# A list planner that counts column loads of W longer and joins the two halves of some DMA transposes

## The chip, the cores and the metric

The kernel runs on one core of a Trainium2 chip, in one launch. Its time is in device microseconds; lower is better. Five instruction queues of the core matter here: TensorE (PE) for matmuls, VectorE (DVE), ScalarE (ACT), GpSimd (POOL), and SyncE (SP), which does no arithmetic and issues every DMA of the kernel.

## What is computed

For each of two batches, `x` is 1024 x 2048 and `ctx` is 2048 x 2048, both float32:

```python
x = x + _L0_xattn_ref(_layernorm(x, axis=-1), ctx_4096, L0_xattn_x1_scale, ...)
x = x + _L0_ffn_ref(_layernorm(x, axis=-1), L0_ffn_W_base, L0_ffn_b_base, ...)
```

The first step quantizes both operands to 8 bits with a scale and a zero point, brings them back, and multiplies them (1024 x 2048 by 2048 x 2048). The second is a linear layer with W (2048 x 2048) and a bias, plus a mixture of 8 experts of rank 16: a router takes the softmax of 8 logits for each token, keeps the best two, and the weighted low-rank products are added.

## The kernel before: tiles, stages and its planner

**The work.** 128 tokens make a tile, so a batch has 8 tiles, worked on in 4 pairs p. Batch 0's first matmul (line 755, into banks `g`) is plain; batch 1's (line 875, `gX` and `gY`) and the FFN matmul of both batches (line 1320, `X` and `Y`) use Strassen's scheme with 7 products of half matrices in place of 8. The FFN operands are each split into two float16 parts, high and low, and three products of parts are summed, so line 1320 issues three matmuls of 128 x 512 a step. The FFN is walked in blocks: for the column half cp of W (f = 0, 1), for the group grp (0 to 3) of Strassen products, for the row block k (0 to 7) of W, for the pair p.

**y.** After the first matmul, `ln2` and `y_prep` (lines 888 to 977) make the seven half sums of normalized x (`yt_...`), split each into a high part by a cast (line 939) and a low part by a subtraction (line 942) in `nat_...` (shape 128 x 2 x 1024), and turn each part by a DMA transpose on SP (`transpose`, line 385) into `y_...`. In the profile the seven appear as `nat_a`/`y_a` and `nat_s`/`y_s`. The low part is made from the high part, so its transpose can be issued one subtraction later at the earliest. Both readers of y, `g2` (line 1311) and `hmm` (line 979, banks `ph`), need both parts. Two other places transpose in two halves: `ln1` for tiles 4 to 7 of batch 0 (`at<-qn`), and `router` (`hT<-hh`). Batch 1's `q<-q` is one transpose for a tile already.

**W.** `w_step` (line 1108) loads what a block needs of W, forms the Strassen combination on VectorE, casts it on ScalarE or VectorE (`affine`, line 396) with the scale gW, and makes the low part on VectorE (line 1130). Row loads, `load_wrow` (`wt`, `wb`), take 128 rows of 1024 consecutive values. Column loads, `load_wcol` (line 570), take the same 512 KB as two pieces of 512 values from two row blocks: `wc` for groups 0 and 2 of f = 0, and all 16 `wn` loads of each `w_norm` (line 579). `w_norm(cp)` squares and sums a column half of W on ScalarE or VectorE (lines 591 and 593), adds the partitions by a matmul (`wsum`, line 604), and computes gW and the factors that undo it (lines 610 to 617, on VectorE); no cast of that half of W can start before.

**The planner.** The program doesn't issue in source order. Each call of `plan.add` makes a Task with its engine (or a choice of ScalarE and VectorE), a modelled duration, what it reads and writes, and for matmuls a due time. `rank` (line 158) passes due times back to predecessors, taking off the duration and a slack (3.0 for a DMA); the modelled DMA time isn't in it. `order` (line 171) then simulates the queues with these numbers, picks for each free engine the ready task with the earliest due time whose buffers fit, and finally sorts all tasks by modelled start. Each engine then runs its part of the list strictly in that order, and semaphores make it wait where the chip differs from the model.

A DMA of n bytes a partition is modelled as `n * 128 / RATE` on one shared channel (`dma_free`), with 0.42 us on SP, landing 2.1 us (`LAND`) after its channel time. SP issues a DMA only while the channel is booked at most `DEPTH` = 2.5 us ahead and fewer than 8 transfers are in flight (`lanes`). A transpose of a half is 1.5 us on SP and 1.0 on the channel; transfers in flight take places of a ring of 5, a half takes 2, and SP is held until there is room:

```python
if t.turn:
    room = RING - TURN_RING
    for at, n in sorted(lanes, reverse=True):
        room -= n
        if room < 0:
            end = max(end, at)
            break
```

Of the kernel before, what the change touches and what calls it, by code (L numbers as in the profile page):

```python
# [22 lines left out]
P = 128  # L23
# [10 lines left out]
C = 512  # L34
NC = O // C
HD = D // 2
# [45 lines left out]
HOP = 0.7  # L82
DMA_SLACK = 3.0
RATE = 374e3
LAND = 2.1
STORE_LAND = 1.15
TURN_LAND = 0.65
TURN_COST = 1.0
TURN_ISSUE = 1.5
RING = 5  # L90
TURN_RING = 2
NEXT = {"DVE": 0.08, "ACT": 0.1}

# [14 lines left out]
class Task:  # L108
    __slots__ = ("eng", "dur", "durs", "fn", "preds", "succs", "prio", "cap", "bufs", "left",
                 "ready", "start", "done", "dma", "seq", "pe", "far", "need", "turn",  # L110
                 "store")


class Plan:
# [4 lines left out]
    def add(self, eng, dur, fn, r=(), w=(), prio=None, cap=None, dma=None, far=None, turn=False,  # L119
            store=False):  # L120
        t = Task()
        t.durs = eng if isinstance(eng, dict) else {eng: dur}
        t.eng, t.dur = None, min(t.durs.values())
        t.fn, t.prio, t.cap, t.dma = fn, prio, cap, dma
        t.preds, t.succs, t.bufs = set(), [], []
        t.seq, t.ready, t.start, t.done = len(self.tasks), 0.0, None, None
        if self.lead is not None:
            t.cap = self.lead
        t.pe = prio if eng == "PE" else None
        t.far, t.turn, t.store = far, turn, store  # L130

        def spans(accs):
            for a in accs:
                buf, parts = a if isinstance(a, tuple) else (a, None)
                if buf not in t.bufs:
                    t.bufs.append(buf)
                    buf.users += 1
                for i in range(buf.parts) if parts is None else parts:
                    yield buf, i

        for buf, i in spans(r):
            last, readers = buf.state[i]
            if last is not None:
                t.preds.add(last)
            readers.append(t)
        for buf, i in spans(w):
            last, readers = buf.state[i]
            if last is not None:
                t.preds.add(last)
            t.preds.update(readers)  # L150
            buf.state[i] = (t, [])
        t.preds.discard(t)
        for p in t.preds:
            p.succs.append(t)
        self.tasks.append(t)
        return t
# [14 lines left out]
    def order(self):  # L171
        self.rank()
        free = dict(SLOTS)
        busy = dict.fromkeys(("SP", "ACT", "DVE", "POOL", "PE"), 0.9)
        ready = {e: [] for e in busy}
        events = [0.0, 0.9]
        lanes = []
# [45 lines left out]
        while todo:  # L223
            if not events:
                raise RuntimeError("no progress")
            nxt = heapq.heappop(events)
            if nxt <= now:
                continue
            now = nxt
            while releases and releases[0][0] <= now:  # L230
                free[heapq.heappop(releases)[-1].tag] += 1
            for eng in busy:
                while busy[eng] <= now:
                    pick = None
                    q = ready[eng]
                    for n, item in enumerate(q):
                        t = item[2]
                        if t.ready > now:
                            continue
                        h = t.far if t.far is not None else HORIZON  # L240
                        if t.prio + lag > now + h:
                            wake(t.prio + lag - h)
                            if t.prio + lag > now + HORIZON:
                                break
                            continue
                        if t.dma is not None:
                            if dma_free > now + DEPTH:
                                wake(dma_free - DEPTH)
                                break
                            if len([x for x in lanes if x[0] > now]) >= LANES:  # L250
                                break
                        if (eng == "DVE" and len(t.durs) > 1 and busy["ACT"] <= now
                                and t.prio > -100):
                            continue
                        if not fits(t):
                            continue
                        pick = t
                        break
                    if pick is None:
                        break  # L260
                    t = pick
                    t.eng, t.dur = eng, t.durs[eng]
                    for e in t.durs:
                        ready[e].remove((t.prio, t.seq, t))
                    for tag, n in t.need.items():
                        free[tag] -= n
                        queue[tag].remove(t)
                    held.update(t.bufs)
                    t.start = now
                    end = now + t.dur  # L270
                    if t.dma is not None:
                        if t.turn:
                            room = RING - TURN_RING
                            for at, n in sorted(lanes, reverse=True):
                                room -= n
                                if room < 0:
                                    end = max(end, at)
                                    break
                        dma_free = max(end + 0.2, dma_free) + t.dma
                        t.done = dma_free + (  # L280
                            TURN_LAND if t.turn else STORE_LAND if t.store else LAND
                        )
                        lanes = [x for x in lanes if x[0] > now]
                        lanes.append((t.done, TURN_RING if t.turn else 1))
                    else:
                        t.done = end + 0.1
                        end -= NEXT.get(eng, 0.0)
                    busy[eng] = end
                    wake(end)
                    wake(t.done)  # L290
                    if t.pe is not None:
                        lag = now - t.pe
                    for b in t.bufs:
                        b.users -= 1
                        if b.tag in free:
                            b.last = max(getattr(b, "last", 0.0), t.done)
                            if not b.users:
                                heapq.heappush(releases, (b.last, next(count), b))
                                wake(b.last)
                    for s in t.succs:  # L300
                        s.left -= 1
                        s.ready = max(s.ready, t.done)
                        if not s.left:
                            for e in s.durs:
                                bisect.insort(ready[e], (s.prio, s.seq, s))
                            wake(s.ready)
                    todo -= 1
        return sorted(self.tasks, key=lambda t: (t.start, t.seq))


@with_exitstack
def xattn_ffn_kernel(ctx, tc, x, cx, scal, wT, bias, arT, bT, out):
# [65 lines left out]
    bmax_b = fixed(None)  # L378
    scale_b = fixed(None, 2)

    def load(dst, dst_ap, src, nbytes, w, r=(), **kw):
        add("SP", 0.42, lambda: nc.sync.dma_start(dst_ap(), src() if callable(src) else src),
            r=r, w=w, dma=nbytes * P / RATE, **kw)

    def transpose(dst, src, r, w, cols, **kw):
        add("SP", TURN_ISSUE, lambda: nc.sync.dma_start_transpose(dst(), src()),
# [183 lines left out]
    def load_wcol(k, cp, c, n, **kw):  # L570
        s = buf("u", [P, HD], F32, n)
        o = cp * HD + c * C
        load(s, lambda: s.ap().rearrange("p (h c) -> p h c", h=2),
             wT.rearrange("(h k p) n -> k p h n", h=2, p=P)[k][:, :, o : o + C], HD * 4, [s], **kw)
        return s

    kept = {}
# [61 lines left out]
    def ln1(S, b, i):  # L639
# [46 lines left out]
        else:  # L686
# [10 lines left out]
            if not pe_turn:  # L697
                for h in range(2):
                    transpose(
                        lambda h=h: aT.ap()[:, h * HK : (h + 1) * HK, :],  # L700
                        lambda h=h: qn.ap()[:, h * HD : (h + 1) * HD], [(qn, [h])], [(aT, [h])],
                        HD)
        S["at", i] = aT
        if first:
            warm = bank("warm")
# [26 lines left out]
    def load_b(S, b, c):  # L732
        for j in range(4):
            bp = buf("u", [P, 4, C], F16, f"b_{b}_{c}_{j}", 2)
            S["b", c, j] = bp
            for h in range(2):
# [2 lines left out]
                s = buf("u", [P, 2, C], F32, f"bs_{b}_{c}_{j}_{h}")  # L739
                load(s, s.ap,  # L740
                     cx[b, k0 * P : (k0 + 2) * P, c * C : (c + 1) * C].rearrange(
                         "(p k) n -> p k n" if b else "(k p) n -> p k n", p=P), HD * 4, [s])
                u = buf("u8", [P, 2, C], U8, f"u_{b}_{c}_{j}_{h}")
                affine(u.ap, s.ap, HD, [s], [u], scale=r2, bias=z2)
                affine(lambda bp=bp, h=h: bp.ap()[:, h * 2 : h * 2 + 2, :], u.ap, HD, [u],
# [174 lines left out]
    def y_prep(S, b, p):  # L920
# [10 lines left out]
        def emit(o, t):  # L931
# [4 lines left out]
            def turn_half(a):  # L936
# [6 lines left out]
                    n.ap()[:, 1], t.ap(), n.ap()[:, 0], ALU.subtract),  # L943
                r=[t, (n, [0])], w=[(n, [1])])
            turn_half(1)

        def comb(dst, a, c, op):
            add("DVE", 1.22, lambda: nc.vector.tensor_tensor(dst.ap(), a.ap(), c.ap(), op),  # L948
# [63 lines left out]
    def router(S, b):  # L1012
# [71 lines left out]
        for q in range(2):  # L1084
# [2 lines left out]
                lambda ts=ts: hT.ap()[:, ts].rearrange("p t h c -> p (t h) c"),  # L1087
                lambda ts=ts: hh.ap()[:, ts].rearrange("p t h c -> p (t h c)"),
                [hh], [(hT, [q])], HD)

    made = {}
    STORED = {
# [413 lines left out]
```

## Time and profile before

| What | us |
|---|---|
| median of 3 runs | 927.42 |
| lowest and highest run | 926.86, 928.04 |
| profiled execution | 927.01 |
| its span, first to last instruction | 925.2 |
| busy in the span: TensorE, VectorE, ScalarE, GpSimd | 901.1, 708.7, 404.3, 66.1 |
| mean granted TensorE clock | 0.991 |

The profile shows one execution. Busy time is what an engine spent on its instructions, without waits. Names in it are the program's tiles without their numbers; `X L1320` is an instruction of line 1320 that writes tile X. "A <- B: t, n, m" in a view of waits says that A waited t us for B in n places, at most m at once. A row of the timeline is: start, length, engine, line, operation, tiles, count of instructions in a row, and the idle time before. `SPq` is SP's queue: the length of a DMA there is the time that SP was held by issuing it, not the transfer's.

The DMA queue's issues, with the median time from issue to landing in us (the first lines and the transposes):

| Transfer | Count | KB | Issue to landing |
|---|---|---|---|
| bs<-in_cx_dram | 64 | 512 | 10.0 |
| wt<-in_wT_dram | 64 | 512 | 7.3 |
| wn<-in_wT_dram | 32 | 512 | 8.8 |
| wc<-in_wT_dram | 16 | 512 | 6.9 |
| y_s<-nat_s (transpose) | 64 | | 3.5 |
| y_a<-nat_a (transpose) | 48 | | 3.6 |
| at<-qn, q<-q, hT<-hh (transposes) | 8, 8, 4 | | 4.5, 6.3, 3.7 |

### The profile page before, as it was taken

The page shows a single profiled execution, that of the slowest core. Times are in us where ns is not written, and L with a number is a line of the kernel's source. Part 1 is how long each engine was busy: PE and PEld are TensorE (multiplying, and loading weights), DVE is VectorE, ACT ScalarE, POOL GpSimd, SP SyncE. Part 2 cuts the span into 40 slices and gives each one's busy share as a digit, 9 for nine tenths or more (in the row PEclk, how much of TensorE's full clock was granted, in tenths as well). Part 3 has the DMA queues.
Part 4 walks back from the last instruction along what each step waited for, and adds up shares of the span by engine and source line. Part 5 has one row for each costly group of instructions (what it writes and reads, how often), then busy time and mean ns, then how long its engine had stood idle before and what let it go on. Part 6 is the DMA issues. An engine that isn't in the chain of part 4 may idle for free.

```text
span 925.2 us, 12515 instructions
## 1 busy us (share of the span) xinstructions
PE 901.1 (97%) x4514; PEld 432.4 (47%) x4514; DVE 708.7 (77%) x1264; ACT 404.3 (44%) x461; POOL 66.1 (7%) x256
## 2 busy tenths in 40 slices
PE   7999998999999899999999999899999999999998
PEld 5444444474444344444444444546544444444443
DVE  7998899989497874989898997799745354799131
ACT  5999677415064331313597575852300011234000
POOL 0023120000000000001552002000000000000000
PEclk8999998999999999999999999999999999999999
DMA  9999999997999999999999656999997159793021
GB/s 322 386 385 295 314 295 253 172 237 228 224 329 322 341 357 405 336 400 353 323 351 314 201 202 171 242 190 187 298 216 255 57 179 385 267 352 126 12 87 49
DMA packets 224526, 241.03 MB, mean 261 GB/s; under 512 B 146640, under 2 KB 158928, under 8 KB 224464
## 3 DMA queue, kind: packets, MB, share of 16 engines
q1 hardware_dynamic: 224464, 240.24, 85.6%
q8 instruction: 35, 0.57, 0.2%
q14 instruction: 27, 0.22, 0.1%
HBM read 163.65 MB, written 41.94 MB: 222 GB/s over the span
## 4 chain that ended last, share of the span: by engine, by line
PE 71%; DVE 11%; DMA 10%; ACT 4%; issue 2%; POOL 1%; SPq 1%; DVEq 0%; ACTq 0%
PE X L1320 30%; PE Y L1320 24%; PE g L755 6%; DMA wn<-in_wT_dram 4%; PE ph L989 2%; PE gX L875 2%; DMA q<-q 2%; PE gY L875 2%; DVE x L784 2%; PE X L1336 1%; PE ph L993 1%; PE Y L1336 1%; DMA lbs<-in_bT_dram 1%; ACT at L396 1%; DMA wb<-in_wT_dram 1%
## 5 line engine op out<-in xcount | busy, mean ns | idle before, releaser
L1320 PEld LDWEIGHTS <-y_s 128*128 128x128 f16 x1536 | 150.2, 98 | 181.8 <-issue 1.3
L1320 PE MATMUL X<-w,y_s 128*128 128x512 f16 x768 | 206.8, 379 | 0.8 <-DVE w L1130 0.8
L1320 PE MATMUL Y<-w,y_s 128*128 128x512 f16 x768 | 206.8, 379 | 0.0
L1320 PE MATMUL X<-w,y_a 128*128 128x512 f16 x768 | 191.8, 382 | 6.5 <-DVE w L1130 2.6
L1320 PEld LDWEIGHTS <-y_a 128*128 128x128 f16 x1152 | 113.0, 99 | 142.0 <-issue 12.1
L755 PE MATMUL g<-b,at 128*128 128x512 f16 x512 | 113.6, 381 | 4.4 <-ACT at L396 2.3
L1320 PE MATMUL Y<-w,y_a 128*128 128x512 f16 x384 | 104.5, 383 | 0.0
L396 ACT ACTIVATE w<-wb,gW 128x1024 f16<-128x1024 f32 (+1 forms) x47 | 50.3, 1073 | 120.3 <-DVE wb L1191 46.2
L1348 DVE SCALAR_TENSOR_TENSOR xr<-X,uW,xr 128x512 f32<-128x512 f32 x64 | 46.7, 746 | 44.0 <-PE X L1336 24.0
L755 PEld LDWEIGHTS <-at 128*128 128x128 f16 x512 | 49.8, 98 | 64.0 <-issue 3.4
L1130 DVE SCALAR_TENSOR_TENSOR w<-wb,gW,w 128x1024 f16<-128x1024 f32 (+1 forms) x48 | 57.1, 1193 | 8.9 <-ACT w L396 8.8
L1348 DVE SCALAR_TENSOR_TENSOR xr<-Y,uW,xr 128x512 f32<-128x512 f32 x42 | 31.1, 744 | 34.8 <-PE Y L1336 34.6
L396 ACT ACTIVATE b<-u,nz 128x1024 f16<-128x1024 uint8 x40 | 44.7, 1138 | 14.5 <-DVE bt L846 13.8
L446 POOL TENSOR_TENSOR sm<-sm 128x1 f32<-128x1 f32 (+1 forms) x48 | 12.2, 253 | 490.0 <-DVE sm L432 484.0
L396 ACT ACTIVATE w<-wt,gW 128x1024 f16<-128x1024 f32 x16 | 18.0, 1145 | 64.5 <-DVE wt L1177 40.0
L419 DVE BATCH_NORM_STATS2 sm<-x 128x6 f32<-128x512 f32 x64 | 40.9, 682 | 3.1 <-DMA x<-in_x_dram 3.0
L396 ACT ACTIVATE q<-x,sm 128x1024 uint8<-128x1024 f32 x30 | 35.9, 1228 | 12.1 <-POOL sm L655 6.5
L396 ACT ACTIVATE nat_s<-yt_a 128x1024 f16<-128x1024 f32 x28 | 28.8, 1051 | 27.9 <-DVE yt_a L948 23.9
L803 ACT ACTIVATE sq<-x,sm 128x1024 uint8<-128x1024 f32 x32 | 36.4, 1137 | 10.4 <-DVE x L784 10.3
L396 ACT ACTIVATE yt_a<-x,sm 128x1024 f32<-128x1024 f32 x26 | 31.1, 1232 | 20.4 <-POOL sm L916 12.1
L396 ACT ACTIVATE u<-bs,sc,rec 128x1024 uint8<-128x1024 f32 x31 | 38.0, 1232 | 4.3 <-DMA bs<-in_cx_dram 3.6
L875 PEld LDWEIGHTS <-at 128*128 128x128 f16 x256 | 24.9, 98 | 30.9 <-issue 1.4
(189 smaller groups left out, 1177.9 us busy)
## 6 DMA issues: line engine op xcount, KB each, us to landing
bs<-in_cx_dram SPq DMA_DIRECT2D x64, 512.0 KB, 10.0
wt<-in_wT_dram SPq DMA_DIRECT2D x64, 512.0 KB, 7.3
wn<-in_wT_dram SPq DMA_DIRECT2D x32, 512.0 KB, 8.8
x<-in_x_dram SPq DMA_DIRECT2D x30, 512.0 KB, 8.5
spill<-x SPq DMA_DIRECT2D x28, 512.0 KB, 3.6
xr<-spill SPq DMA_DIRECT2D x28, 512.0 KB, 8.3
wb<-in_wT_dram SPq DMA_DIRECT2D x24, 512.0 KB, 8.0
out_dram<-xr SPq DMA_DIRECT2D x24, 512.0 KB, 5.8
```

The source lines that it names most:

```text
L396: nc.scalar.activation(o, i, AF.Copy if c is None else AF.Identity, scale=1.0 if a is None else a, bias=0.0 if c is None else c,)
L419: nc.vector.bn_stats(st[:, 2 * h + c], b.ap()[:, c * C : (c + 1) * C])
L446: e.tensor_tensor(t, r, r, ALU.mult)
L755: nc.tensor.matmul(ps.ap(), aT.ap()[:, k, :], S["b", c, k // 4].ap()[:, k % 4, :], start=k == 0, stop=k == KT - 1,)
L784: nc.vector.scalar_tensor_tensor(xs, ps.ap(), s12, xs, ALU.mult, ALU.add, **kw)
L803: nc.scalar.activation(sq.ap(), xb.ap(), AF.Square, bias=a[:, 22 + j : 23 + j], accum_out=a[:, 24 + 2 * j + h : 25 + 2 * j + h],)
L875: nc.tensor.matmul(ps.ap(), a()[:, 4 * h + k, :], w.ap()[:, k, :], start=fresh and h + k == 0, stop=h == 1 and k == 3, skip_group_check=True,)
L989: nc.tensor.matmul(ph.ap()[:, : 2 * AR], y[half].ap()[:, 0, k, :], ar[:, kr, :], start=kk == 0, stop=False,)
L1130: lambda: nc.vector.scalar_tensor_tensor(w.ap()[:, 1, lo:up], src(), g, w.ap()[:, 0, lo:up], ALU.mult, ALU.subtract),
L1320: nc.tensor.matmul(ps.ap(), y.ap()[:, a, k, :], w.ap()[:, q, j * C : (j + 1) * C], start=k == 0 and fresh and i == 0, stop=k == HK - 1 and ...
L1336: nc.tensor.matmul(ps.ap(), hT.ap()[:, 2 * p + tt, a], lb.ap()[:, q], start=fresh and i == 0, stop=i == 2, skip_group_check=True,)
L1348: nc.vector.scalar_tensor_tensor(xs, ps.ap(), uW[:, cp : cp + 1], xs, ALU.mult, ALU.add)
```

## The change

It has two parts, both in the planner and in what it is told.

1. `load` gets a factor `slow` on the modelled channel time of a DMA: 1.18 for column loads of W (`load_wcol`), 1.03 for loads of cx in `load_b`.
2. The last two transposes added before a call of `pair_up` become mates, with a function that issues one DMA transpose for both halves. When one of them is picked, its mate is ready too, the mate's buffers are held (or are the same), and every transfer in flight lands within `MERGE` = 2.5 us by the model, the two are issued as one: 1.8 us on SP (and SP held until the last transfer in flight has landed), twice the channel time, 4 places of the ring. `pair_up` is called in `ln1`, `y_prep` and `router`.

The core of the diff:

```diff
+SLOW_W = 1.18
+SLOW_C = 1.03
+MERGE = 2.5
+WHOLE_ISSUE = 1.8
...
+                    group = [t]
+                    m = t.mate
+                    if m is not None and m.start is None and not m.left and m.ready <= now:
+                        ok = all(b in held or b in t.bufs or b.tag not in free for b in m.bufs)
+                        if ok and max([x[0] for x in lanes] or [0.0]) < now + MERGE:
+                            group.append(m)
+                            t.dur = WHOLE_ISSUE
+                            t.fn, m.skip = t.whole, True
                     end = now + t.dur
                     if t.dma is not None:
                         if t.turn:
-                            room = RING - TURN_RING
+                            room = RING - TURN_RING * len(group)
                             for at, n in sorted(lanes, reverse=True):
                                 room -= n
-                                if room < 0:
+                                if room < 0 or len(group) > 1:
                                     end = max(end, at)
                                     break
-                        dma_free = max(end + 0.2, dma_free) + t.dma
+                        dma_free = max(end + 0.2, dma_free) + t.dma * len(group)
...
-    def load(dst, dst_ap, src, nbytes, w, r=(), **kw):
+    def load(dst, dst_ap, src, nbytes, w, r=(), slow=1.0, **kw):
         add("SP", 0.42, lambda: nc.sync.dma_start(dst_ap(), src() if callable(src) else src),
-            r=r, w=w, dma=nbytes * P / RATE, **kw)
+            r=r, w=w, dma=nbytes * P / RATE * slow, **kw)
+
+    def pair_up(whole):
+        a, c = [t for t in plan.tasks[-3:] if t.turn][-2:]
+        a.mate, c.mate = c, a
+        a.whole = c.whole = whole
...
+            pair_up(lambda: nc.sync.dma_start_transpose(
+                y.ap().rearrange("p h k t -> p (h k) t"), n.ap().rearrange("p h c -> p (h c)")))
```

The rest of the diff books the group's two tasks together (start, end, buffers, successors) and leaves the skipped one out of the final list.

More of the change, by code (lines that the diff above doesn't have):

```diff
@@ L110 @@
                  "ready", "start", "done", "dma", "seq", "pe", "far", "need", "turn",
-                 "store")
+                 "store", "whole", "mate", "skip")
 class Plan:
@@ L130, in add @@
         t.far, t.turn, t.store = far, turn, store
+        t.whole = t.mate = None
+        t.skip = False
         def spans(accs):
@@ L262, in order @@
                     t.eng, t.dur = eng, t.durs[eng]
[L263 to L269, printed above, removed]
+                    group = [t]
[6 more added lines that the diff above has]
+                            t.fn, m.skip = t.whole, True
                     end = now + t.dur
@@ L272, in order @@
                         if t.turn:
-                            room = RING - TURN_RING
+                            room = RING - TURN_RING * len(group)
                             for at, n in sorted(lanes, reverse=True):
                                 room -= n
-                                if room < 0:
+                                if room < 0 or len(group) > 1:
                                     end = max(end, at)
                                     break
-                        dma_free = max(end + 0.2, dma_free) + t.dma
-                        t.done = dma_free + (
+                        dma_free = max(end + 0.2, dma_free) + t.dma * len(group)
+                        done = dma_free + (
                             TURN_LAND if t.turn else STORE_LAND if t.store else LAND
@@ L283, in order @@
                         lanes = [x for x in lanes if x[0] > now]
-                        lanes.append((t.done, TURN_RING if t.turn else 1))
+                        lanes.append((done, TURN_RING * len(group) if t.turn else 1))
                     else:
-                        t.done = end + 0.1
+                        done = end + 0.1
                         end -= NEXT.get(eng, 0.0)
@@ L289, in order @@
                     wake(end)
-                    wake(t.done)
+                    wake(done)
                     if t.pe is not None:
                         lag = now - t.pe
[L293 to L308, printed above, removed]
+                    for t in group:
+                        t.start, t.done = now, done
+                        for e in t.durs:
+                            ready[e].remove((t.prio, t.seq, t))
+                        for tag, n in t.need.items():
+                            free[tag] -= n
+                            queue[tag].remove(t)
+                        held.update(t.bufs)
+                        for b in t.bufs:
+                            b.users -= 1
+                            if b.tag in free:
+                                b.last = max(getattr(b, "last", 0.0), t.done)
+                                if not b.users:
+                                    heapq.heappush(releases, (b.last, next(count), b))
+                                    wake(b.last)
+                        for x in t.succs:
+                            x.left -= 1
+                            x.ready = max(x.ready, t.done)
+                            if not x.left:
+                                for e in x.durs:
+                                    bisect.insort(ready[e], (x.prio, x.seq, x))
+                                wake(x.ready)
+                        todo -= 1
+        done = [t for t in self.tasks if not t.skip]
+        return sorted(done, key=lambda t: (t.start, t.seq))
 @with_exitstack
@@ L573, in load_wcol @@
         load(s, lambda: s.ap().rearrange("p (h c) -> p h c", h=2),
-             wT.rearrange("(h k p) n -> k p h n", h=2, p=P)[k][:, :, o : o + C], HD * 4, [s], **kw)
+             wT.rearrange("(h k p) n -> k p h n", h=2, p=P)[k][:, :, o : o + C], HD * 4, [s],
+             slow=SLOW_W, **kw)
         return s
@@ L702, in ln1 @@
                         HD)
+                pair_up(lambda: nc.sync.dma_start_transpose(aT.ap(), qn.ap()))
         S["at", i] = aT
@@ L741, in load_b @@
                      cx[b, k0 * P : (k0 + 2) * P, c * C : (c + 1) * C].rearrange(
-                         "(p k) n -> p k n" if b else "(k p) n -> p k n", p=P), HD * 4, [s])
+                         "(p k) n -> p k n" if b else "(k p) n -> p k n", p=P), HD * 4, [s], slow=SLOW_C)
                 u = buf("u8", [P, 2, C], U8, f"u_{b}_{c}_{j}_{h}")
@@ L1089, in router @@
                 [hh], [(hT, [q])], HD)
+        pair_up(lambda: nc.sync.dma_start_transpose(
+            hT.ap().rearrange("p t h c -> p (t h) c"),
+            hh.ap().rearrange("p t h c -> p (t h c)")))
     made = {}
```

## Prediction

> **What bounds the kernel now.** I read the page's busy times first, then TensorE's waits, then windows of time with the granted clock, then single tiles and the DMA queue's timeline.
>
> ```profile
> span 925.2 us, 12515 instructions
> PE 901.1 (97%) x4514; PEld 432.4 (47%) x4514; DVE 708.7 (77%) x1264; ACT 404.3 (44%) x461; POOL 66.1 (7%) x256
> ```
>
> TensorE is busy 97% of the span, so 925.2 - 901.1 = 24.1 us is all that a better order could give back in idle time. The view of TensorE's waits tells where most of it lies:
>
> ```profile
> PE X L1320 <- DVE w L1130: 3.4, 4, 1.4
> PE ph L993 <- DMA y_a<-nat_a: 3.1, 1, 3.1
> PE X L1320 <- ACT w L396: 2.4, 1, 2.4
> ...
> PE wsum L604 <- DVE wacc L600: 1.7, 1, 1.7
> PE X L1320 <- DVE x L1348: 1.5, 1, 1.5
> ```
>
> By time (TensorE's timeline) these make three places. **At 147**: idle 2.39, one matmul, idle 1.44, because the scale gW of the W norm is late. **From 277 to 317**: 0.78 + 1.49 + 0.17 + 1.73 + 0.98 = 5.15, in the stage that loads W for batch 0. **At 586**: 3.06, waiting for a transposed y half. Some 6 us more lie in the first 28 us; elsewhere TensorE runs without a wait, but for 0.7 us at 532. Two of the three cost more than their idle time; the windows show it in the granted clock (columns: stretch, length, busy time and count of PE, PEld, DVE, ACT, POOL, PEclk, DMA share, GB/s):
>
> ```profile
> 151.00:157.00 6.00, 5.87 (x15) 2.07 (x15) 6.00 (x7) 6.00 (x9) 0.00 (x0) 0.51 1.10 273
> 586.00:589.00 3.00, 0.16 (x2) 0.00 (x0) 2.98 (x7) 1.34 (x4) 0.00 (x0) 1.00 1.12 281
> 589.00:592.00 3.00, 2.78 (x24) 2.34 (x25) 2.01 (x9) 2.62 (x4) 0.00 (x0) 0.74 1.10 217
> 592.00:595.00 3.00, 3.00 (x22) 2.11 (x20) 0.99 (x6) 1.45 (x3) 0.00 (x0) 0.69 1.03 190
> 308.00:311.00 3.00, 1.27 (x8) 0.54 (x6) 0.36 (x2) 1.76 (x3) 0.00 (x0) 1.00 1.02 410
> ```
>
> After the idle time at 147 the clock is 0.51 for 6.00 us: 6.00 x 0.49 = 2.9 us lost, so that place costs 3.83 + 2.9 = 6.8. After 586: 3.00 x 0.26 + 3.00 x 0.31 = 1.7, in all 4.8. After the 1.73 us before 310.6 the clock stays 1.00. [...]
>
> **Part 1: column loads counted longer.** It adds and removes no instruction. Only the order in which the planner lists tasks can change, and what each queue then waits for. Modelled time of a 512 KB load: 4096 x 128 / 374e3 = 1.40 us; with SLOW_W 1.65, with SLOW_C (cx) 1.44. 32 wn and 16 wc loads x 0.25 = 12.1 us of modelled queue time, 64 cx loads x 0.042 = 2.7. Is that nearer to the chip? Windows where column loads are nearly alone, and where row loads and stores are:
>
> ```profile
> 254.00:281.00 27.00, 26.22 (x122) 11.73 (x120) 24.49 (x60) 14.91 (x23) 0.00 (x0) 1.00 0.99 335
> 325.00:345.00 20.00, 20.00 (x94) 9.04 (x93) 14.56 (x18) 6.57 (x6) 0.00 (x0) 1.00 1.03 366
> ```
>
> 335 GB/s against 366, where the model has 374 for all: columns deserve 374 / 335 = 1.12, rows 1.02. From each DMA record's issue and landing, two wn loads in a row land 1.35 us apart (median of 18), but between 254.1 and 280.4 sixteen of wn and wc land 1.76 apart on average, some gaps being 2.2 to 3.4. So 1.65 lies between a quiet queue and this stage: better here, too long elsewhere. What the planner's optimism costs is seen in a tile:
>
> ```profile
> who waited for it (us, times):
>   ACT wn L591: 41.8, 13
>   PE X L1320: 3.8, 2
> ```
>
> ScalarE stands 41.8 us in front of squares of wn whose load has not landed, with casts of w queued behind them (5.0 us before 303.10, then a cast of w at 304.16). Counted longer, squares come later in ScalarE's order and the w casts ahead of them. Of the five idle times of 277 to 317, three hang on column loads: 0.78 (w from wc), 1.73 (wsum before the last wn has landed), 0.98 (the w step behind the wsum chain on VectorE). I take these as gone: -3.49. The other 1.66 wait for row loads wb, whose cost is not changed. Bounds: -5.15 if all go, 0 if none. A loss is not excluded: 16 wn loads between 95 and 129 are modelled 16 x 0.25 = 4.0 us later, and gW at 147 hangs on them (rival D). In the stage at 586 three wc loads stand on SP just ahead of the transposes; one fewer there would bring y forward by one landing (1.35 to 3.15 apart), at most the whole 4.8. I count 0 for it: nothing fixes which comes first.
>
> **Part 2: joined halves.** SP's timeline shows where halves stand in a row:
>
> ```profile
> 223.44 2.61 SPq L386 DMA_TRANSPOSE y_s<-nat_s  x2
> ...
> 233.60 14.64 SPq L386 DMA_TRANSPOSE y_s<-nat_s  x10
> ```
>
> Two free halves hold SP 2.61 us; a lone half holds it 1.23 and lands 3.1 after its issue. The trace has no whole one, so its SP time lies between 1.23 (it costs like a half) and 2.61 (like two); the planner has 1.8, and I take that, so 0.8 saved each. Both consumers (g2, hmm) need both halves, so a whole delays none of them by itself. Where both halves are ready together (16 halves in 223 to 248, 16 in 657 to 688), TensorE waits for no y: the cover is matmul work on y halves that landed long before. At 577 to 588, where TensorE does wait, the second half of nat is written 1.2 us (one subtraction) after the first and SP is not behind. So the saving is worth 0 on the path; ends: 0.8 x 2 pairs there = -1.6, and +5.0 if a whole blocks SP (rival E). [...]
>
> **Sum.** Against the profiled execution (927.01 us, 1.8 more than its span): -3.49 + 0 = 923.5. The median of the runs, 927.42, is 0.41 above it: **923.9 us**.
>
> **Rivals.** All move with one fact: the planner's list is made anew, and three short places decide.
>
> **A, the forecast** (0.35): the three column waits go, the rest stays. 923.9; its own range 922 to 926.
>
> **B, a long stall goes too** (0.15): with gW's chain or the y half moved up, 147 (6.8) or 586 (4.8) vanishes with its half clock. For it: wsum was ready at 135.3 (wacc reduced) but stands on TensorE at 142.10, and VectorE takes it up only at 146.44, behind two Newton chains. Against: these are placed by due times, which the change leaves. 917.1 to 919.1; both, 912.3.
>
> **C, no difference** (0.12): the changed orders lie where TensorE has cover (157 to 277, 317 to 586, 595 to 920), or merges hardly occur. 927.4.
>
> **D, gW comes later** (0.16): the wn loads count 4.0 us longer, the planner puts wsum that much later, and TensorE, out of other work at 146.9, idles on. +4.0: 931.4. It decides from the point where 4.0 exceeds the slack between the last square (130.1, by ScalarE's timeline) and the reduction at 135.26: 5.1 us now, which speaks against it.
>
> **E, a whole transpose blocks SP** (0.22): the half at 577.94 held SP 4.58 us with 4 transfers in flight, the one at 117.94 6.87 with 7, against 1.3 free. A whole is planned where little is in flight by the model, but at 576.6 real loads landed up to 6.2 us later. One whole held 3.3 us longer just ahead of a y that TensorE waits for makes an idle time of 3.3 and, as after 586, 1.7 of clock: +5.0, 932.4; by the longer hold, 5.6 + 2.9 = +8.5, 935.9. It decides where more than two halves' worth is really in flight at the issue.
>
> Slower than before is thus D + E = 0.38, faster A + B = 0.50, within 0.2% C = 0.12 (0.2%, some 1.9 us, is about what a measurement can tell from no change). Both signs hold much, so the range runs from B's far part to E's: 914 to 936.
>
> **What would show it.** In the profile after: A, the waits of X and wsum between 277 and 317 shrink from 5.15 to about 1.7 and ScalarE's wait for wn falls well below 41.8. B, no clock of 0.5 after 147 or 586. D, the first X later than 149.31. E, a long DMA_TRANSPOSE on SP followed by a wait of PE for y. Part 2: fewer than 132 transposes, whole ones holding SP 1.23 to 2.61. Wrong would make me above all a new stall beyond 3 us at a place that has none now, for it takes the clock with it.

## The result, and the profile after

The changed kernel takes 917.85 us (median of 4 runs, 917.43 to 918.72), the kernel before 927.73 beside it (926.86 to 930.37): a ratio of 0.9887, 95% interval 0.9868 to 0.9907. It is faster by 9.9 us; forecast were 3.5. The sign was right and the time lies in the range, but the size was nearly three times the forecast. What follows asks where the other 6 us come from.

The head of the page of after (span 915.7; the profiled execution took 917.52):

```profile
span 915.7 us, 12485 instructions
PE 897.4 (98%) x4514; PEld 431.3 (47%) x4514; DVE 712.6 (78%) x1271; ACT 399.9 (44%) x454; POOL 67.1 (7%) x256
```

TensorE's idle time was 24.1 and is 915.7 - 897.4 = 18.3; its busy time fell by 3.7, with the same 4514 matmuls. Half of that is half clock: in before's profile TensorE worked 13.2 us at a clock of 0.51 (in 16.9 to 23.9, 150.1 to 157.0 and 590.4 to 593.9), which lost 6.4, in after's 9.3 us (in 19.5 to 26.4 and 149.2 to 152.7), which lost 4.5. The rest isn't traced. TensorE's waits in after:

```profile
PE ph L1018 <- DMA y_a<-nat_a: 4.1, 2, 3.4
...
PE ph L1014 <- DMA y_a<-nat_a: 2.3, 2, 2.0
...
PE X L1348 <- DVE w L1158: 0.7, 1, 0.7
PE X L1348 <- ACT w L417: 0.5, 1, 0.5
```

(Line numbers moved: 993 is now 1018, 989 is 1014, 1320 is 1348, 1130 is 1158, 396 is 417, 604 is 626.) The waits of X for w, 3.4 + 2.4 before, are 0.7 + 0.5; the wait of wsum (1.7) and that for x (1.5) are gone. What is left are transposed y halves: 2.02 + 0.73 at 145.5 to 148.6, where gW was late before, and 3.36 at 577.8. In the windows (columns as in the prediction):

```profile
144.00:149.00 5.00, 2.25 (x23) 1.66 (x24) 4.83 (x16) 4.94 (x6) 0.00 (x0) 1.00 1.15 198
149.00:152.00 3.00, 3.00 (x16) 1.74 (x15) 2.66 (x4) 1.96 (x4) 0.00 (x0) 0.54 1.03 195
...
577.00:581.00 4.00, 0.82 (x5) 0.20 (x2) 3.86 (x12) 2.81 (x5) 0.00 (x0) 1.00 1.03 244
581.00:590.00 9.00, 8.68 (x76) 6.12 (x77) 4.95 (x15) 6.66 (x9) 0.00 (x0) 1.00 1.02 204
```

After the idle time at 147 the clock is again 0.54; after the longer one at 577.8 it stays 1.00.

**The stage from 254 to 340.** The greatest difference is here. The tile wn in after, as it was read before (41.8 us then; both figures are of the whole span, in 250 to 325 alone they are 22.0 and 12.2):

```profile
  ACT wn L613: 19.2, 13
```

ScalarE's wait fell well below 41.8, as forecast. The lists of ScalarE and VectorE differ too. Before, ScalarE makes every cast of w in 250 to 325; in after VectorE makes four of them, three of wc and one of wb (tile w in this stretch, first before, then after):

```profile
L396 ACT ACTIVATE w<-wc,gW x6: 1132/1132/1148, 257.3 to 283.9; 128x1024 f16<-128x1024 f32 x6
```

```profile
L424 DVE TENSOR_SCALAR w<-wc,gW x3: 744/746/752, 260.3 to 279.4; 128x1024 f16<-128x1024 f32 x3
```

Another queue shows more of why TensorE's operands were late: SP itself. Its waits between 250 and 325, first before, then after:

```profile
SPq L382 <- DMA wn<-in_wT_dram: 20.8, 7, 7.4
SPq L382 <- ACT wn L591: 10.0, 8, 1.9
```

```profile
SPq L398 <- DMA wn<-in_wT_dram: 7.4, 5, 3.9
SPq L398 <- ACT wn L613: 6.3, 7, 1.2
```

SP issues its list in order. A load needs a free buffer of the shared pool; where that buffer still holds an earlier wn whose load has not landed, or has not been squared, SP stands, and with it every load behind. Before, the wait for a landing took 7.4 us at a stretch. SP's timeline of before shows the hole:

```profile
295.40 0.33 SPq L382 DMA_DIRECT2D wb<-in_wT_dram  x1
304.28 0.38 SPq L382 DMA_DIRECT2D wn<-in_wT_dram  x1
304.75 0.42 SPq L382 DMA_DIRECT2D wt<-in_wT_dram  x1
```

Nothing is issued for 8.5 us, the wt load behind wn goes out 0.47 us after it, and then the queue has run dry: in 304 to 312 the DMA share is 0.80. The load that stood is the last wn of the norm: issued at 304.28 it lands at 309.14, and wsum, for which TensorE stands idle, goes at 310.63. In after the last wn lands at 303.74. In after no gap in SP's issues between 287 and 306 is over 4 us. What reached the core between 295 and 305, before and then after:

```profile
295.00:305.00 10.00, 8.51 (x41) 3.76 (x39) 9.24 (x14) 3.63 (x6) 0.00 (x0) 1.00 0.91 340
```

```profile
295.00:305.00 10.00, 10.00 (x48) 4.55 (x47) 9.58 (x13) 3.74 (x6) 0.00 (x0) 1.00 1.03 409
```

340 GB/s against 409, and TensorE busy 8.51 us against all 10.00.

**The joined halves.** 17 pairs became one (132 transposes before, 115 after), 4 on y_a and 13 on y_s. On the y halves, in the tile nat_a of after (min/median/max in ns on SP):

```profile
L407 SPq DMA_TRANSPOSE y_a<-nat_a x40: 1231/1470/8710, 104.1 to 625.4; - x40
...
L969 SPq DMA_TRANSPOSE y_a<-nat_a x4: 1982/2129/2472, 139.4 to 580.1; - x4
```

### The profile page after: what moved, and what is told of

Same layout as the page of the kernel before. It is cut to its first block, busy times and chain, and to the rows that moved or that the text cites. A ratio compares the mean times of both kernels' runs of the same rounds, so it can differ in the third digit from the quotient of the medians.

```text
span 915.7 us, 12485 instructions
## 1 busy us (share of the span) xinstructions
PE 897.4 (98%) x4514; PEld 431.3 (47%) x4514; DVE 712.6 (78%) x1271; ACT 399.9 (44%) x454; POOL 67.1 (7%) x256
## 4 chain that ended last, share of the span: by engine, by line
PE 86%; DVE 7%; DMA 4%; issue 1%; POOL 1%; SPq 0%; ACT 0%; DVEq 0%
PE X L1348 36%; PE Y L1348 27%; PE g L778 6%; PE gX L898 5%; PE gY L898 4%; PE ph L1014 2%; PE X L1364 2%; PE Y L1364 2%; DMA bs<-in_cx_dram 1%; PE ph L1018 1%; DMA wn<-in_wT_dram 1%; DVE x L807 1%; DMA y_a<-nat_a 1%; DVE nat_a L965 1%; DMA wc<-in_wT_dram 1%
## 5 line engine op out<-in xcount | busy, mean ns | idle before, releaser
L1348 PE MATMUL X<-w,y_a 128*128 128x512 f16 x768 | 189.9, 380 | 1.2 <-DVE w L1158 0.7
L778 PEld LDWEIGHTS <-at 128*128 128x128 f16 x512 | 49.9, 99 | 64.7 <-issue 4.5
L417 ACT ACTIVATE w<-wt,gW 128x1024 f16<-128x1024 f32 x14 | 16.1, 1148 | 63.6 <-DVE wt L1205 37.2
L417 ACT ACTIVATE yt_a<-x,sm 128x1024 f32<-128x1024 f32 x28 | 33.4, 1231 | 23.4 <-POOL sm L939 13.7
L1018 PE MATMUL ph<-ar,y_a 128*128 128x136 f16 x192 | 35.3, 225 | 4.2 <-DMA y_a<-nat_a 4.1
```

What stands on the lines that cost most here:

```text
L417: nc.scalar.activation(o, i, AF.Copy if c is None else AF.Identity, scale=1.0 if a is None else a, bias=0.0 if c is None else c,)
L778: nc.tensor.matmul(ps.ap(), aT.ap()[:, k, :], S["b", c, k // 4].ap()[:, k % 4, :], start=k == 0, stop=k == KT - 1,)
L1018: nc.tensor.matmul(ph.ap()[:, AR : 2 * AR], y[half].ap()[:, 1, k, :], ar[:, kr, :AR], start=False, stop=kk == KT - 1,)
L1348: nc.tensor.matmul(ps.ap(), y.ap()[:, a, k, :], w.ap()[:, q, j * C : (j + 1) * C], start=k == 0 and fresh and i == 0, stop=k == HK - 1 and ...
```

## The experiments

**Theories.** T1: the gain is the column factor's, and lies in the stage of 254 to 340, where SP no longer stands on wn. T2: it is the joined halves. T3: no part matters for what it says; any new list re-deals three short places, and this one was a good deal. T4: it is the place of one task, wsum or its scale. Ratios are against the kernel before, run beside each. The profile columns come from one execution each: "SP" is SP's longest wait for a landing of wn between 250 and 325, "wsum" TensorE's wait there, and the last three say how much later (+) or earlier TensorE gets through a place than in the first profile of before: 147 (from hmm's first matmul at 136 to the 50th FFN matmul), the stage (from the 400th to the 720th, 254 to 340 in before), 586 (from the end of batch 1's first matmul at 584 into its FFN). "W", "cx" and "J" are the column factor of W, the factor of cx and the joined halves.

| Run | Ratio [95%] | SP | wsum | 147 | stage | 586 |
|---|---|---|---|---|---|---|
| before | | 7.4 | 1.7 | 0 | 0 | 0 |
| after (W, cx, J) | 0.9887 [0.9868, 0.9907] | 3.9 | none | -2.07 | -4.70 | -1.05 |
| e1 (W, cx) | 0.9921 [0.9899, 0.9943] | 2.1 | none | -2.70 | -2.21 | +1.39 |
| e2 (J) | 0.9977 [0.9960, 0.9995] | 8.7 | 2.5 | -1.49 | +0.50 | -1.65 |
| e3 (W) | 0.9908 [0.9885, 0.9931] | 3.3 | none | -4.30 | -2.62 | +0.51 |
| e12 (W, J) | 0.9889 [0.9870, 0.9908] | 4.3 | none | -3.98 | -3.03 | +0.68 |
| e4 (all loads x 1.023) | 0.9962 [0.9948, 0.9976] | 3.0 | 0.2 | -3.37 | -1.71 | +1.60 |
| e5 (all x 1.003) | 0.9978 [0.9964, 0.9992] | 6.8 | 2.1 | -5.54 | +2.36 | +0.89 |
| e6 (all x 0.997) | 0.9998 [0.9982, 1.0015] | 8.0 | 1.9 | -2.25 | +2.89 | +0.60 |
| e7 (gW moved up) | 1.0051 [1.0031, 1.0071] | 7.9 | 2.3 | -7.46 | +3.57 | +0.46 |
| e8 (second wsum down) | 1.0007 [0.9992, 1.0023] | 7.3 | moved | -0.79 | +3.55 | +0.22 |
| e9 (W in the second norm) | 0.9945 [0.9928, 0.9962] | 4.0 | none | +0.05 | +0.60 | +0.52 |
| e10 (W in the first norm) | 0.9980 [0.9966, 0.9993] | 6.4 | 1.7 | -4.74 | +1.26 | -0.47 |
| e11 (W in wc) | 0.9965 [0.9953, 0.9976] | 3.9 | none | -1.81 | -1.57 | +1.21 |
| e14 (W 1.09, cx, J) | 0.9945 [0.9926, 0.9963] | 4.0 | none | -1.57 | -1.40 | -2.14 |
| e15 (W 1.27, cx, J) | 0.9969 [0.9949, 0.9988] | 3.4 | none | -3.75 | -2.99 | +1.50 |
| e13 (before again) | one run, 928.86 us | 8.5 | 1.9 | -2.21 | +3.70 | +0.16 |
| e16 (after again) | one run, 917.14 us | 4.0 | 0.3 | -3.63 | -3.29 | -1.59 |

**e1, e2, e3: one part alone.** The edits in after: e1 and e3 never join, e2 has no factors.

```diff
-MERGE = 2.5
+MERGE = -1e6       # e1, e3
-SLOW_C = 1.03
+SLOW_C = 1.0       # e2, e3
-SLOW_W = 1.18
+SLOW_W = 1.0       # e2
```

> The changed kernel without joined halves (no pair is ever joined), the longer column and cx loads kept. Theory 1 (the gain is the truer cost of column loads): 916 to 920 us, TensorE's idle time between 277 and 317 falls from 5.15 to about 1.2 as in the changed kernel. Theory 2 (the gain is the joined halves): 925 to 929. Theory 3 (any newly made list would do; the size is chance): somewhere between 915 and 935, with idle times at other places.

> Joined halves alone, all loads counted as before. Theory 1: 925 to 929, the idle time between 277 and 317 stays near 5. Theory 2: 916 to 920. Theory 3: between 915 and 935.

> Only the 48 column loads of W counted 1.18 times as long; cx as before, nothing joined. Theory 1: 916 to 921, the stage 250 to 321 as in the changed kernel. Theory 2: 925 to 929. Theory 3: between 915 and 935, and not the same as the run that counts cx longer too.

Measured: 0.9921, 0.9977 and 0.9908. The column factor alone brings 927.4 x 0.0092 = 8.5 us, with cx beside it 7.3 (the intervals overlap: cx adds nothing that shows), the joined halves alone 2.1. In e2 the stage is as before, SP's wait and that of wsum included:

```profile
SPq L398 <- DMA wn<-in_wT_dram: 21.9, 8, 8.7
```

```profile
PE wsum L626 <- DVE wacc L622: 2.5, 1, 2.5
```

In e3 both are gone:

```profile
SPq L398 <- DMA wn<-in_wT_dram: 8.6, 6, 3.3
```

T2 falls as the main cause. But e3's 8.5 are not the stage's alone: against the mean of before's two profiles (the second is e13) they are some 4.5 in the stage and 3.2 at 147.

**e4, e5, e6: a longer load of any kind, or merely another list.** In before:

```diff
-RATE = 374e3
+RATE = 365.6e3     # e4; e5: 373e3, e6: 375e3
```

> The kernel before with every DMA counted 2.3% longer (RATE 365.6e3), which adds about the same modelled queue time in all (14.8 us) but doesn't set columns apart. Theory 1: 925 to 929, since columns still cost what rows cost. Theory 2: 925 to 929. Theory 3: moves by several us either way, like the others.

> The kernel before with RATE 373e3 in place of 374e3: every DMA counted 0.3% longer, a change without meaning, to see how far any newly made list moves the time. Theory 1 (truer column cost): 927 to 929, the idle time between 277 and 317 near 5. Theory 3 (any new list): off by 2 us or more from the kernel before, mostly to the faster side if the list of before was an unlucky one at 147.

> The same with RATE 375e3: every DMA counted 0.3% shorter. Theory 1: 927 to 929. Theory 3: 2 us or more off, and not the mirror image of the run with longer loads.

A change of 0.3%, which says nothing about columns, gave 0.9978 and 0.9998: a mere re-deal of the list was worth 0.2 to 2.0 us in these two (T3 had expected 2 or more of each). That is the measure for T3, and the 2.1 of the joined halves alone cannot be told from it. 8.5 to 9.9 can. All loads longer by 2.3% gave 0.9962, SP's longest wait falling to 3.0: counting every load longer shortens the same wait, and in the stage one profile can't tell it from e3 (-1.71 and -2.62); the whole gains 3.5 us in place of 8.5. That columns had to be set apart for the stage, no run shows.

**e7, e8: single tasks moved by hand in the list of before.** e7 puts the first wsum, its scale and the casts of two w steps earlier; e8 the second wsum 8 TensorE tasks later.

```diff
-        for task in plan.order():
+        tasks = plan.order()
+        r, s, f = [marks[x, 0] for x in ("red", "sum", "fin")]
+        early = marks["hi"][:2] + marks["lo"][:2]
+        for x in [s, f] + early:
+            tasks.remove(x)
...
+        after = {dve[2]: [f] + marks["hi"][:2], dve[4]: marks["lo"][:2]}
...
+        for task in tasks:
```

```diff
+        s, f = marks["sum", 1], marks["fin", 1]
+        at = tasks.index(s)
+        later = [t for t in tasks[at + 1:] if t.eng == "PE"][8]
+        tasks.remove(s)
+        tasks.insert(tasks.index(later) + 1, s)
```

> The list of before, with seven tasks moved by hand and nothing planned anew: the wsum matmul of the first W norm right behind its reduction, the scale gW three VectorE tasks behind that, and the first two W steps' casts and low parts behind gW and two more VectorE tasks. If the stall at 147 comes from the order of these tasks (behind two Newton chains), its 3.83 us idle and 2.9 us of half clock go: 921 to 923. If it only moves on to the next late thing (y of the last pair, 3 us as in the changed kernel), 924 to 926. If the order doesn't matter there: 928.

> The list of before, with the wsum matmul of the second W norm moved eight TensorE tasks (24 matmuls, 5.2 us) down, and its scale behind it. If the 1.73 us before wsum are the price of its place in TensorE's order, they go and nothing comes: 926 to 926.5. If the loads are simply late there, the wait comes back at the next matmul: 928; if the scale is then late for the next block, slower, 929 to 930.

e7 removed the stall at 147 (-7.46 there), but TensorE now stood 3.31 us for wacc at 131.5, with half clock behind it: +6.59 ahead of 147, in all 1.0051, slower than any of the three times expected. The wait changed its place. In e8 the wait of wsum became one of X for w at 316, 2.10 us, and the ratio is 1.0007, as expected if the loads are simply late. Where wsum stands is not the price; that its operands come late is. T4 falls.

**e9, e10, e11: which column loads.** In e3, the factor for one group alone (e10: `wn_0`, e11: `wc`):

```diff
-             slow=SLOW_W, **kw)
+             slow=SLOW_W if n.startswith("wn_1") else 1.0, **kw)
```

> Counted longer (1.18): only the 16 wn loads of the second W norm (issued between 249 and 304 before). The list up to there is that of before. Theory 1a (between 277 and 317 SP stood 8.5 us without an issue, 295.7 to 304.3, because the buffer of its next wn load was held by a wn load that landed later than planned; counted longer, the planner puts other loads ahead of that wait): the stage 250 to 324 gains 3 to 5 us, SP's longest wait for a wn landing falls from 7.4 to under 4, no wait of wsum; total 922 to 925, and 147 and 586 as before. If the 48 columns work only together or by another list at 147: 927 to 929.

> Counted longer: only the 16 wn loads of the first W norm (93 to 129). Theory 1b: gains 2 to 5 us at 147 as the other new lists did there, the stage 250 to 324 keeps its wait of wsum near 2; total 924 to 927. Rival D of the prediction: gW comes 4 us later, 930 to 932.

> Counted longer: only the 16 wc loads. Theory 1: little, 925 to 929, as the long wait on SP is for wn, though four of them stand between 250 and 278. Theory 3: anything between 920 and 930.

Gains of 5.1, 1.9 and 3.2 us (927.4 x 0.0055, 0.0020, 0.0035); their sum, 10.2, is a little over e3's 8.5. The second norm, whose 16 wn loads lie in the stage, is the largest, and takes SP's longest wait from 7.4 to 4.0. In its one profile the stage was no faster (+0.60, with a wait of 3.49 for w at 278 and half clock for 3.5 us behind it); that execution, 927.23, was also the slowest of its six. The first norm's 1.9 is again no more than a re-deal. The 3.2 of wc are more than the little that T1 expected.

e9 and e11 change less than it seems. By the tiles in the traces, every queue's list is that of before up to 257; SP issues the same kinds of transfer in the same order up to 323 and 319, TensorE's matmuls up to 311 and 316. What differs before that is VectorE and ScalarE alone: in the stage VectorE takes six and three casts of w. Yet SP's longest wait falls to 4.0 and 3.9, in e11 without one wn load counted longer. So the order of SP's own list is not what made it stand. Which load stands changes with the buffer that it is given: in e9 it is a row load (issued at 301.00) that in before went out at 294.16, ahead of the hole.

**e12: without the cx factor.**

```diff
-SLOW_C = 1.03
+SLOW_C = 1.0
```

> The changed kernel without the longer cx loads: columns of W and joined halves. If the parts add up (columns alone -8.9, joined alone -2.4): 916 to 918. If joined halves do harm beside the longer columns: 919 to 922.

0.9889 against 0.9887: the cx factor did nothing that shows. The parts add up: 8.5 of e3 and 2.1 of e2 against 10.3 here (927.4 x 0.0111). So up to 2 us may be the joined halves', which cannot be told from a re-deal.

**e13, e16: the same lists once more; e14, e15: other factors.** e13 is before and e16 after, unedited.

```diff
-SLOW_W = 1.18
+SLOW_W = 1.09      # e14; e15: 1.27
```

> The list of before, unchanged, profiled a second time, as a measure of how far one profile of one list is from the next. If single profiles are good to 0.5 us per place, the idle times come back within 0.5 us each: 147 with 2.4 + 1.4 and the half clock, wsum 1.7, 586 with 3.1. If the DMA-limited stage differs from execution to execution, the stage from 254 to 329 moves by 1 to 3 us with the same list, and only differences of the medians may be read.

> Whole change with SLOW_W 1.09 in place of 1.18. If the factor acts as a dose (the closer the model is to the stage's 1.76 us a load, the less SP stands), the time lies between that of joined halves alone (ratio 0.998) and that of the whole change (0.989), at 0.993 to 0.995, and SP's longest wait for a landing of wn lies between 8.7 and 3.9 us. If what counts is that the list is another one, it falls anywhere between 0.988 and 1.002.

> Whole change with SLOW_W 1.27. As a dose: 1.27 x 1.40 = 1.78 us a load, the mean distance of landings measured in the stage, so SP's longest wait for wn is at most 3.9 us and the ratio 0.989 or a little below. If chance of a new list: anywhere between 0.988 and 1.002, with the longest wait of SP for wn free to be over 6 us.

> The list of after, unchanged, profiled a second time. Good to 0.5 us per place: SP's wait for wn landings 7.4 us in sum and 3.9 at most, no wait of wsum, 147 with 3.0 idle and half clock. If executions differ, the idle at 147 or at 577 moves by over 1 us, or the half clock there comes or goes with the same idle time.

*One profile is not the kernel.* The list of before, profiled again, is 3.70 us slower in the stage and 2.21 faster at 147:

```profile
PE X L1320 <- DVE w L1130: 6.3, 5, 2.2
...
PE wsum L604 <- DVE wacc L600: 1.9, 1, 1.9
```

X waits 6.3 for w in place of 3.4. TensorE's idle time in the stage is 8.66 (1.20 + 2.20 + 1.43 + 0.45 + 0.41 + 1.87 + 1.10), not 5.15. e7 and e8, which leave nearly all of that stage's list as it was, show +3.57 and +3.55 too. So the profile that the prediction was made from had an unusually quick stage. In after again, the idle time at 147 is 1.94 + 0.55, and no half clock follows:

```profile
149.00:152.00 3.00, 3.00 (x20) 1.55 (x18) 3.00 (x5) 2.87 (x5) 0.00 (x0) 1.00 1.07 184
```

*The factor works in its stage, and beyond 1.09 its size shows little there.* SP's longest wait is 4.0, 3.9 and 3.4 for 1.09, 1.18 and 1.27. Over all 18 profiles, the ten whose longest SP wait is at most 4.3 have a mean stage of -2.29 us (-4.70 to +0.60), the eight with 6.4 or more +2.23 (0 to +3.70): 4.5 us lie between them. These are not 18 independent lists: the eight leave every cast of w in 250 to 325 to ScalarE, each of the ten gives VectorE one to six. SP's wait and this split go together in every run, so which of the two makes the gain stays open. As far as the stage goes, this speaks for T1. *But the whole time does not follow the factor*: 0.9945, 0.9887, 0.9969. At 1.27 the stage is as good (-2.99 against -4.70 and -3.29), and the list loses elsewhere. Batch 1's first matmul waits for its half sums at 491 and 502, and after 3.49 idle at 581 the clock is halved:

```profile
PE gX L898 <- DVE as L852: 1.7, 2, 1.2
```

```profile
586.00:590.00 4.00, 4.00 (x21) 2.56 (x20) 0.00 (x0) 0.94 (x1) 0.00 (x0) 0.50 1.04 199
```

At 1.09 a wait for x of 2.06 at 299 costs a half clock of its own (below). So T3 is the best reading of the rest: 1.18 is not on a slope that could be followed, it is the value whose lists are good at most places at once. The four lists with 1.18 on all columns (after, e12, e3, e1) lie at 0.9887 to 0.9921, every other one at 0.9945 or above. None of the versions beat after; e12 equals it.

## Why the prediction was right in sign and short in size

Two steps failed. The term of the column waits was too small (3.49; the stage gave 5.85), and 147, 340 to 586 and 586 were put at 0 (they gave 1.75, 1.47 and 1.40). The total of 917.85 lies where rival B stood (917.1 to 919.1), but by many places, not by one long stall that vanished.

| Place | Forecast | Two profiles of after against two of before |
|---|---|---|
| 147 | 0 | -2.85 + 1.10 = -1.75 |
| stage, 254 to 340 | -3.49 | -4.00 - 1.85 = -5.85 |
| 340 to 586 | 0 | -1.36 - 0.11 = -1.47 |
| 586 | 0 | -1.32 - 0.08 = -1.40 |

(Means of the last column; with the small rest they make 10.6, the medians 9.9.)

- **The column waits of 277 to 317 go: right, and the main term.** 0.78 and 1.73 are gone in after, 0.67 for a low part of w stays at 311.75, and 1.18 of idle time is left in all (1.73 in the second profile; forecast 1.66). The term was mis-sized: 5.85 for 3.49. Its base was one profile with 5.15 idle, where the second had 8.66. The reason given, ScalarE's order, was a part of it: casts of w did leave ScalarE's path, though to VectorE and not merely ahead of the squares. It left out SP's own wait, 20.8 in that stretch. "Is that nearer to the chip?" was answered too well: two wn loads in a row land 1.35 us apart, less than the 1.40 of the model without a factor, so 1.65 is a margin for the gaps in this stage's landings and not a column load's price. The wait for x (1.49), which I kept because row loads are counted as before, is gone in both profiles of after, and in every list with 1.18 or more on any columns, but stands in e14 (2.06): why is open. That the SP wait and the casts go with the gain is shown by the 18 profiles; what each causes alone is not, since no run moves only those casts or gives the list of before one buffer more.
- **147 and 586 counted as 0: the step that failed.** "These are placed by due times, which the change leaves" was the argument for 147. The runs show that a new list shortens it. Before's own list up to there was profiled five times (before, e13, e8, e9, e11): 0, -2.21, -0.79, +0.05 and -1.81, mean -0.95. The eleven lists that the planner made anew ahead of 147 are at -1.49 to -5.54, mean -3.3 (after by its two profiles). The stall of before was thus no fixed point but mostly an unlucky one, and rival B (0.15 for one such place) deserved more. It went only in part: in after gW is no longer what TensorE waits for, and y halves of a pair took its place.
- **586.** The place did not vanish: 3.06 idle became 3.36 (3.14). The gain is the half clock (1.7 by the prediction's price): it follows in both profiles of before and in none of after. That is luck as far as the runs tell: with 3.36 idle there, e1 has half clock for 6.9 us and after for none, and e12, with after's gain, has it too (3.73 idle, 3.5 us). At 340 to 586, where I saw cover but for 0.7 at 532, that wait went; the rest of the 1.47 isn't traced.
- **Part 2 worth 0: right within what can be told.** Alone 0.9977, as much as e5's re-deal. Its price: a whole transpose issued at 222.16 with nothing in flight held SP 2.00 us and landed 4.30 after its issue; two free halves at 223.44 held it 2.61, the second landing 4.47 after the first's issue. So 0.6 is saved there, not the 0.8 taken, and the whole is neither a half (1.23) nor two (2.61): it held SP for three quarters (0.77) of the two.
- **Rival D did not come.** The first X is indeed later in after's first profile (150.43 against 149.31) but behind y halves and with more hmm work done ahead of it; the 50th FFN matmul is 2.07 earlier. With only the first norm counted longer (e10), 147 gained 4.74.
- **Rival E did not come.** Where it was to decide, at more than two halves' worth in flight, is an estimate; by before's DMA records, 53 halves issued with two transposes and no other transfer in flight held SP 1.23 to 2.03 us, eight with one transpose and three other transfers 1.77 to 4.58. The four wholes on y_a held SP 1.98 to 2.47. Three of the 13 on y_s held it longer than the sign's 2.61 (2.96 to 3.20), but TensorE waits for no y_s. The waits of 2.02 and 0.73 at 147 stand in e1 too, which joins nothing (1.93 and 0.62). The wait at 577.8 hangs on two halves issued from 575.60, ahead of any whole there (580.10).
- **The clock's price.** That a stall beyond 3 us takes the clock with it, as the 3.06 of before did, was no rule: the 3.36 and 3.14 of after's two profiles at 578 did not (see the end). In the whole, the mean granted clock is 0.991 over the 95 runs of before beside the experiments and 0.994 over after's five; of the span that is 8.4 and 5.7 us, idle time at half clock included, so the clock makes at most some 2.7 of the 9.9 us.
- **A small sum.** The first 28 us hold 7.1 us of idle time, not some 6; no term rests on it.

## What to carry to other kernels

Where one queue issues every load in order, read that queue's own waits before those of the engines: a load that stands for a buffer delays all behind it, whatever their kind (8.5 us without an issue here), and a planner that counts loads too short for a crowded stage (1.40 us where landings were 1.76 apart) plans with buffers that are not free yet. When a change makes a list anew, every place that idles by accident is dealt again, so count those places in the forecast with a chance each, not as fixed. And size a term from two profiles of the kernel before where DMA sets the pace: here one list gave 5.15 and 8.66 us for the same stage.

## What the hardware showed beside this

**Between 2.06 and 3.36 us, the length of an idle time did not decide whether half clock follows.** In e14, 2.06 us idle at 299 were enough:

```profile
301.00:304.50 3.50, 3.35 (x8) 1.16 (x8) 3.50 (x6) 1.34 (x2) 0.00 (x0) 0.52 1.01 372
```

In after, 3.36 and 3.14 at 578 were not, 3.36 at 580 in e1 was, and the same place of one list (147 in after) had it in one execution (2.02 + 0.73 idle) and not in the other (1.94 + 0.55). At the stall at 578 to 586 all eight idle times of 3.49 us and more were followed by it, none of 2.79 and less. What decides in between, no run here shows.

**Half clock came in two lengths, 3.5 and 6.9 us.** Between the first 30 us and the last matmul, each stretch of it in the 18 profiles lasts one or the other, which at the 0.51 of the rows below costs 1.7 or 3.4 where TensorE has work throughout, less where it idles in part:

```profile
150.10:157.00 6.90, 5.87 (x15) 2.07 (x15) 6.90 (x7) 6.90 (x10) 0.00 (x0) 0.51 1.06 259
```

```profile
149.20:152.70 3.50, 3.50 (x16) 1.85 (x14) 3.16 (x5) 2.46 (x4) 0.00 (x0) 0.51 1.04 198
```

```profile
581.80:588.70 6.90, 5.69 (x30) 3.90 (x31) 1.15 (x9) 2.28 (x2) 0.00 (x0) 0.51 1.07 212
```

(Before, after and e1.)
